# Edge sums by products with a matrix of the ends, all weights loaded at once, and a score behind layer 2's operands, in a kernel of four graph layers

## The chip, the cores and the metric

The kernel runs on one core of one Trainium2 chip; no other core runs a part of it. The metric is device time in microseconds (us) of one launch; less is better. Every comparison below sets runs of a kernel against runs of the kernel before on the same chip, taken in the same rounds.

Engines, as the profile names them: PE is TensorE's products, PEld its weight loads, DVE is VectorE, ACT is ScalarE, POOL is GpSimd, SP issues DMAs.

## The reference, cut to what matters

128 graphs of 128 nodes with 256 features pass four layers; each adds its result to its input and normalizes. All is float32. Layer 0 is attention along 512 edges, and the change's first part is in it:

```python
Xq = (H @ W_lin.T).reshape(bt, n, h, dh)
Qs = Xq[:, src]                     # the queries of each edge's one end
Kt = Xq[:, dst]                     # and of its other end
e = jnp.einsum('behd,hd->beh', leaky_relu(Qs + Kt, 0.2), a)
e = e + jnp.log(A0[src, dst] + EPS)[None, :, None]
...                                 # softmax over the edges of each source
Y = segment_sum(attn[..., None] * Vt, src, num_segments=n)
```

Layer 1 is three products by weights w1, w2, w3, each followed by a mixing of the nodes. Layer 2 is the change's third part: three weights for the diagonal, the upper and the lower part of the adjacency.

```python
h = jnp.einsum('bjf,kfo->kbjo', x, W)
out = adj_0 @ h[0] + adj_1 @ h[1] + adj_2 @ h[2] + bias
```

Layer 3 is two products with batch norms over all graphs.

## The kernel before: the parts that matter

The graphs go in 32 quads of four, through a software pipeline. A function `start` brings the first quads to the point where the pipeline is full; then each iteration does the attention of one quad, layer 1 of an earlier one, layers 2 and 3 of one earlier still. The order of the calls is the order in each engine's queue, and an operation waits for those in front of it there: in the prediction below, an operand whose input is there at 372.4 us is made at 375.67, after the score that stands before it.

A score of one chunk of 128 edges is three VectorE passes over 128x1024, 3.65 us together. Its input, the sum of the queries at both ends, comes by two gathers from the quad's queries in HBM, the second with an add:

```python
def gather_one(k, t, c):
    s = quads[k]
    idx, op = ((src_idx, ALU.bypass), (dst_idx, ALU.add))[t]
    nc.gpsimd.indirect_dma_start(out=s.z[c], ..., in_=s.qd, in_offset=...idx[:, c:c + 1]..., compute_op=op)

def score(k, c):
    ...
    nc.vector.scalar_tensor_tensor(z, z, SLOPE, z, op0=ALU.mult, op1=ALU.max)
    nc.vector.tensor_mul(z3, z3, a_bc...)
    nc.vector.reduce_sum(s.es[:, c, :], ...)
    if c == NE - 1:
        nc.vector.tensor_add(s.es, s.es, log_col...)
```

The edges are sorted by source for the softmax's scans: `perm` is a 0/1 matrix of the sorting, and the sorted indices are products with it. The gathers use those, so they have to wait for them.

The attention of a quad is scattered to HBM and read back as a matrix `ad`; `by_row` copies it into the order that the aggregation's products need, by ScalarE or, in the start, by ScalarE and VectorE in turn:

```python
def by_row(k, j, copy=None):
    ...
    (copy or nc.scalar.copy)(s.adc[:, j * H:(j + 1) * H, :],
                             s.ad.rearrange("p (s r) -> p r s", r=R)[:, j * H:(j + 1) * H, :])
```

Layer 2 is a generator. Its operands (`mix`: two products, one ScalarE copy, and `ms`, a VectorE multiplication) are made for one graph at a time, its products (`prod`) follow:

```python
mix(0)
mix(1)
yield
prod(0)
yield
mix(2)
prod(1)
yield
mix(3)
layer_norm(...)
prod(2)
yield
prod(3)
layer_norm(...)
```

The first step (up to the first `yield`) is taken at the end of the iteration before. An iteration then takes two more steps, a score, and the rest, so that the score stands between `prod(1)` and `mix(3)`:

```python
parts = quads[a].layer2 if a > 0 else iter(())
next(parts, None)
next(parts, None)
if has_e:
    score(e, 0)
    gather_last(e)
for _ in parts:
    pass
```

Of the kernel before, what the change touches and what calls it, by code (L numbers as in the profile page):

```python
# [8 lines left out]
F32 = mybir.dt.float32  # L9
# [16 lines left out]
def gnn_stack(ctx: ExitStack, tc: tile.TileContext, x, adj, w_qv_t, a, w_out_t, src, dst,  # L26
# [101 lines left out]
    with ExitStack() as phase:  # L128
        cst = phase.enter_context(tc.tile_pool(name="cst", bufs=1))

        class Quad:
            pass

# [107 lines left out]

        def values(k, i, copy=None, queue=None):

            copy = copy or nc.vector.tensor_copy
            s = quads[k]
            if i == 0:
                s.qt = wk.tile([P, QB, D], F32, tag="xb", name=f"qt{k}", bufs=1)
                s.xv = ws.tile([P, QB, D], F32, tag="xv", name=f"xv{k}", bufs=3)
            pq = ps("pq")
            for c in range(DC):  # L250
                nc.tensor.matmul(pq, s.xts[i // 2][:, i % 2, c, :], wqv[:, c, :], start=(c == 0), stop=(c == DC - 1))
            nc.scalar.copy(s.qt[:, i, :], pq[:, :D])
            copy(s.xv[:, i, :], pq[:, D:])
            if i == QB - 1:
                spill(k, queue)

        def spill(k, queue=None):
            s = quads[k]
            s.qd = q_dram[k % 4]
            (queue or nc.sync).dma_start(s.qd, s.qt.rearrange("p b d -> p (b d)"))  # L260

# [46 lines left out]

        def gather(k, z=None, chunks=range(NE - 1)):


            s = quads[k]
            s.z = z or {}
            for c in chunks:
                if c not in s.z:
                    s.z[c] = z_buffer(k, c)
            jobs = [(t, c) for t in range(2) for c in chunks]
            if k == 0:
                jobs = [(0, 0), (0, 1), (1, 0), (0, 2), (1, 1), (0, 3), (1, 2), (1, 3)]
            for t, c in jobs:  # L320
                gather_one(k, t, c)

        def z_buffer(k, c):
            return ws.tile([P, QB * D], F32, tag="zs", name=f"zs{k}_{c}", bufs=NE - 1)
# [12 lines left out]

        def score(k, c):

            s = quads[k]  # L340
            if c == 0:
                s.es = ws.tile([P, NE, R], F32, tag="es", name=f"es{k}", bufs=1)
            z = s.z[c]
            nc.vector.scalar_tensor_tensor(z, z, SLOPE, z, op0=ALU.mult, op1=ALU.max)  # L344
            z3 = z.rearrange("p (b d) -> p b d", d=D)
            nc.vector.tensor_mul(z3, z3, a_bc.unsqueeze(1).to_broadcast([P, QB, D]))  # L346
            nc.vector.reduce_sum(s.es[:, c, :], z.rearrange("p (r d) -> p r d", d=DH), axis=AX.X)  # L347
            if c == NE - 1:
                nc.vector.tensor_add(s.es, s.es, log_col.unsqueeze(2).to_broadcast([P, NE, R]))

        def softmax_parts(k):

            s = quads[k]
            pe = ps("pe")
            for c in range(NE):
                nc.tensor.transpose(pe[:R, c * P:(c + 1) * P], s.es[:, c, :], ident)
            f = wk.tile([R, E], F32, tag="f", name="f", bufs=1)
# [431 lines left out]
        def iteration(k):  # L789
# [6 lines left out]
            parts = quads[a].layer2 if a > 0 else iter(())  # L796
            next(parts, None)
            next(parts, None)
            if has_e:
# [143 lines left out]
        def start():  # L943
# [24 lines left out]
            adj_idx = wk.tile([P, NE], I32, tag="adj_idx", name="adj_idx", bufs=1)  # L968
            nc.vector.scalar_tensor_tensor(adj_idx, ends[:, 0, :], float(N), ends[:, 1, :], op0=ALU.mult, op1=ALU.add)
            key_row = scratch("key_row")  # L970
            nc.vector.scalar_tensor_tensor(key_row, rows_i[0], float(E), pos, op0=ALU.mult, op1=ALU.add)
# [13 lines left out]

            quads[1].xr = load_x(1)
            nc.sync.dma_start(att_dram[0][:N * N, :].rearrange("(t s) r -> t (s r)", s=N), zero)
            nc.sync.dma_start(wo, w_out_t.rearrange("(c p) f -> p c f", p=P))
            values_in(0, quads[0].xr, nc.scalar.copy)
            for i in range(QB):  # L990
                values(0, i, nc.scalar.copy, nc.scalar)
            quads[2].xr = load_x(2)

            def sorted_columns(t):
                pc = ps("pcol")[:, :NE * 2].rearrange("p (c t) -> p c t", t=2)
                for c in range(NE):
                    for i in range(NE):
                        nc.tensor.matmul(pc[:, c, :], perm[:, i, c * P:(c + 1) * P], ends[:, t:t + 2, i],
                                         start=(i == 0), stop=(i == NE - 1))
                return pc  # L1000

            pc = sorted_columns(0)
            nc.vector.tensor_copy(src_idx, pc[:, :, 0])
            nc.vector.tensor_copy(dst_idx, pc[:, :, 1])
            gather(0, {NE - 1: l2w.rearrange("p k c f -> p (k c f)")[:, :QB * D]}, range(NE))
            pr = ps("src_row")
            for c in range(NE):
                nc.tensor.matmul(pr[:R, :], src_wide[:, c, :], perm[:, c, :], start=(c == 0), stop=(c == NE - 1))
            src_row = scratch("src_row")
            nc.scalar.copy(src_row[:R, :], pr[:R, :])  # L1010

            values_in(1, quads[1].xr, nc.scalar.copy)
            for i in range(QB):
                values(1, i, nc.scalar.copy, nc.scalar)
            z2 = zpool.tile([P, 2, QB * D], F32, tag="z", name="z_1", bufs=1)
            gather(1, dict(enumerate((z2[:, 0, :], z2[:, 1, :], w2t.rearrange("p c d -> p (c d)"),
                                      l3w1.rearrange("p c f -> p (c f)")))), range(NE))

# [16 lines left out]
            nc.vector.tensor_add(ends[:, 2, :], weight, pair_col)  # L1035

            pc = sorted_columns(2)


# [4 lines left out]

            xg3 = load_x(3, "xg", 1, ws)

            for c in range(NE):
                score(0, c)
                if c == 1:
                    nc.vector.tensor_copy(att_idx, pc[:, :, 0])  # L1050
                    nc.vector.tensor_copy(log_col, pc[:, :, 1])
            steps = softmax_parts(0)
            for _ in range(2):
                next(steps)
            values_in(2, quads[2].xr, nc.scalar.copy)
            next(steps)
            values(2, 0, nc.scalar.copy)
            values(2, 1, nc.scalar.copy)
            for _ in steps:
                pass  # L1060
            attention(0)
            for i in (2, 3):
                values(2, i, nc.scalar.copy)
            scatter(0)
            nc.sync.dma_start(w1_sb, w1.rearrange("(c p) f -> p c f", p=P))
            nc.sync.dma_start(w2_sb, w2.rearrange("(c p) f -> p c f", p=P))
            nc.sync.dma_start(att_dram[1][:N * N, :].rearrange("(t s) r -> t (s r)", s=N), zero)
            nc.sync.dma_start(w3_sb, w3.rearrange("(c p) f -> p c f", p=P))
            nc.sync.dma_start(l2w, l2_w.rearrange("k (c p) f -> p k c f", p=P))
            nc.sync.dma_start(bias, bass.AP(tensor=l2_bias.tensor, offset=l2_bias.offset, ap=[[0, P], [1, D]]))  # L1070
            for t, vecs in ((bn1, (l3_b1, l3_g1, l3_be1)), (bn2, (l3_b2, l3_g2, l3_be2))):
                for i, ap in enumerate(vecs):
                    nc.sync.dma_start(t[:, i, :], ap.rearrange("(c p) -> p c", p=P))

# [31 lines left out]

            values_in(3, xg3, nc.scalar.copy)
            gather(2)
            for c in range(NE - 1):
                score(1, c)  # L1110
            for j in range(QB):
                by_row(0, j, nc.vector.tensor_copy if j % 2 else None)
            aggregate(0)
            stage_a(0)
            for i in range(QB):
                values(3, i, nc.scalar.copy)
            quads[4].xg = load_x(4, "xg", 1, ws)
            score(1, NE - 1)
            nc.sync.dma_start(l3w1, l3_w1_t.rearrange("(c p) f -> p c f", p=P))
            nc.sync.dma_start(w2t, l3_w2_t.rearrange("(c p) f -> p c f", p=P))  # L1120
            mix1(0, 0)
            mix1(0, 2)
            steps = softmax_parts(1)
            first(0, 0)
            next(steps)
            second_sums()
            for i in range(QB):
                if i + 1 < QB:
                    first(0, i + 1)
                mix2(0, i)  # L1130
                next(steps, None)

        with tc.manual_schedule(engines=None):
# [305 lines left out]
```

## Time and profile before

| quantity | before |
|---|---|
| time, median of 3 runs | 3249.05 us (3248.92 to 3249.43) |
| span of the profiled run | 3252.2 us |
| TensorE busy | 3137.4 us, 96% |
| VectorE busy | 2145.3 us, 66% |
| ScalarE busy | 1276.3 us, 39% |
| TensorE waits for layer 2's operand `ms` | 33.9 us in 29 waits |

How to read it: with TensorE at 96%, anything that isn't TensorE's work can give back roughly the missing 115 us, and only if TensorE waits for it. It helps to cut the span into four parts by rows of TensorE's timeline. *Start* ends where the first row of the second product of layer 1 begins (109.99 us before). *Iteration 0* lasts until the same row of iteration 1. *Middle* lasts until the plain hidden products of the last quad. *Tail* is the rest, two batch norms whose code isn't touched. Before, the four are 109.99, 90.78, 2725.97 and 325.46 us.

The profile's lines that carry the argument are in the prediction below.

### The profile page before, as it was taken

To read this page: it belongs to the slowest core of one execution; us is meant where nothing else is said; L and a number is where in the kernel's file an instruction comes from. 1 tells how busy PE (TensorE), PEld (TensorE's weight loads), DVE (VectorE), ACT (ScalarE), POOL (GpSimd) and SP (SyncE) were. 2 spreads that over 40 slices of the span, in tenths; PEclk is the share of its full clock that TensorE was granted. 3 is DMA by queue.
4 is the path that set the end of the run, shared out by engine and by line. 5 is a ranking of instruction groups with operands and counts; after the bars stand their busy time and mean duration, and the time that the engine had idled before them with its cause. 6 is when DMAs were issued, how large, how long until landed. Compare 5 with 4: busy or idle time off the path is not lost. (4 is left out here: it accounts for less than half of the span.)

```text
span 3252.2 us, 41204 instructions
## 1 busy us (share of the span) xinstructions
PE 3137.4 (96%) x15884; PEld 2590.5 (80%) x15884; DVE 2145.3 (66%) x4200; ACT 1276.3 (39%) x2229; POOL 644.1 (20%) x541
## 2 busy tenths in 40 slices
PE   6999999999999999999999999999999999999997
PEld 3788888888888888888888888888888888874444
DVE  6666666666666666666666666666666666437878
ACT  2343333333333333333333333333333333326668
POOL 4211222212111111222112111112222111001125
PEclk7999999999999999999999999999999999999999
DMA  7613333333333223333333333233333331005557
GB/s 219 174 52 92 104 98 104 93 96 105 95 95 99 84 79 98 105 98 104 92 98 104 86 103 93 78 88 101 98 104 101 94 92 53 20 24 178 176 192 272
DMA packets 118756, 344.86 MB, mean 106 GB/s; under 512 B 15008, under 2 KB 51744, under 8 KB 110240
## 3 DMA queue, kind: packets, MB, share of 16 engines
q0 software_dynamic: 45552, 151.55, 19.4%
q1 hardware_dynamic: 70960, 188.71, 16.2%
q8 instruction: 126, 2.06, 0.3%
q10 hardware_dynamic: 2048, 1.97, 0.2%
q14 instruction: 70, 0.57, 0.1%
HBM read 256.20 MB, written 85.98 MB: 105 GB/s over the span
## 5 line engine op out<-in xcount | busy, mean ns | idle before, releaser
L535 PE MATMUL ph<-m,w 128*128 128x256 f32 x2048 | 464.2, 380 | 0.0
L616 PE MATMUL p<-w,h 128*128 128x256 f32 x2048 | 462.3, 379 | 0.0
L616 PEld LDWEIGHTS p<-w,h 128*128 128x128 f32 x2048 | 389.2, 190 | 65.9 <-issue 7.6
L535 PEld LDWEIGHTS ph<-m,w 128*128 128x128 f32 x2048 | 387.6, 190 | 51.4
L329 POOL DMA_INDIRECT zs<-qd,src_idx x123 | 119.6, 972 | 1443.7 <-DVE z L739 884.0
L666 PE MATMUL po<-l2w,ms 128*128 128x256 f32 x1536 | 355.7, 382 | 33.9 <-DVE ms L658 33.9
L535 PE MATMUL ph<-m,w_s 128*128 128x256 f32 x1536 | 352.4, 379 | 0.0
L666 PEld LDWEIGHTS po<-l2w,ms 128*128 128x128 f32 x1536 | 282.7, 190 | 78.7 <-DVE ms L658 45.4
L535 PEld LDWEIGHTS ph<-m,w_s 128*128 128x128 f32 x1536 | 291.9, 190 | 39.6
L112 ACT ACTIVATE ln_sd<-ln_mv,eps 128x2 f32<-128x2 f32 x192 | 56.3, 293 | 514.2 <-DVE ln_mv L107 514.1
L329 POOL DMA_INDIRECT zs<-qd,dst_idx x123 | 192.5, 1565 | 258.2 <-DMA zs<-qd,src_idx 246.9
L548 DVE TENSOR_TENSOR h<-ph,u 128x512 f32<-128x512 f32 x128 | 88.1, 689 | 167.6 <-PE ph L535 114.3
L389 POOL DMA_INDIRECT attd<-at,att_idx x128 | 126.1, 985 | 361.4 <-DMA attd<-at,att_idx 252.8
L542 ACT COPY u<-ph 128x512 f32<-128x512 f32 x128 | 74.9, 585 | 245.1 <-PE ph L535 245.1
L346 DVE TENSOR_TENSOR zs<-zs,a_bc 128x1024 f32<-128x1024 f32 x123 | 150.6, 1225 | 4.2
L347 DVE TENSOR_REDUCE es<-zs 128x16 f32<-128x1024 f32 x123 | 150.0, 1220 | 4.2
L344 DVE SCALAR_TENSOR_TENSOR zs<-zs 128x1024 f32<-128x1024 f32 x123 | 149.5, 1215 | 2.4 <-DMA zs<-qd,dst_idx 2.4
L120 DVE TENSOR_SCALAR xr<-xr,ln_mv,ln_rs 128x256 f32<-128x256 f32 x384 | 145.1, 420 | 6.9
L105 DVE BATCH_NORM_STATS2 ln_st<-xr 128x6 f32<-128x256 f32 x384 | 144.2, 417 | 5.5
L654 ACT COPY ms<-pm 128x512 f32<-128x512 f32 x128 | 71.1, 579 | 194.4 <-PE pm L652 191.0
L477 DVE TENSOR_TENSOR h<-z,adc 128x512 f32<-128x512 f32 x62 | 41.9, 675 | 153.9 <-ACT adc L471 153.8
L640 POOL TENSOR_TENSOR xb<-xr,bias 128x512 f32<-128x512 f32 x64 | 81.6, 1275 | 293.1 <-DVE xr L120 155.2
(298 smaller groups left out, 5706.9 us busy)
## 6 DMA issues: line engine op xcount, KB each, us to landing
ad<-attd SPq DMA_DIRECT2D x32, 1024.0 KB, 4.8
zd<-z SPq DMA_DIRECT2D x31, 1024.0 KB, 7.4
zl<-zd SPq DMA_DIRECT2D x62, 512.0 KB, 3.6
xr<-in_x_dram SPq DMA_DIRECT2D x32, 512.0 KB, 5.9
x3d<-xr SPq DMA_DIRECT2D x32, 512.0 KB, 5.4
x3l<-x3d SPq DMA_DIRECT2D x32, 512.0 KB, 5.1
out_dram<-x3l POOLq DMA_DIRECT2D x31, 512.0 KB
qd<-qt SPq DMA_DIRECT2D x30, 512.0 KB, 2.6
```

The costliest lines, as they stand in the source:

```text
L105: nc.vector.bn_stats(st[:, i, :], r[:, i, :])
L120: nc.vector.tensor_scalar(r[:, i, :], r[:, i, :], mv[:, i, 0:1], rs[:, i:i + 1], op0=ALU.subtract, op1=ALU.mult)
L329: nc.gpsimd.indirect_dma_start(out=s.z[c], out_offset=None, in_=s.qd, in_offset=bass.IndirectOffsetOnAxis(ap=idx[:, c:c + 1], axis=0), com ...
L344: nc.vector.scalar_tensor_tensor(z, z, SLOPE, z, op0=ALU.mult, op1=ALU.max)
L346: nc.vector.tensor_mul(z3, z3, a_bc.unsqueeze(1).to_broadcast([P, QB, D]))
L347: nc.vector.reduce_sum(s.es[:, c, :], z.rearrange("p (r d) -> p r d", d=DH), axis=AX.X)
L389: nc.gpsimd.indirect_dma_start(out=ad, out_offset=bass.IndirectOffsetOnAxis(ap=att_idx[:, c:c + 1], axis=0), in_=s.at[:, c, :], in_offset= ...
L535: nc.tensor.matmul(bank[g][:, i].rearrange("p b n -> p (b n)"), wa[:, c, f:f + P], s.m2[:, blk_b, c].rearrange("p b n -> p (b n)"), start= ...
L548: nc.vector.tensor_add(block(g, row, col), bank[g], kept_[g])
L616: nc.tensor.matmul(p3[:, t * D:(t + 1) * D], s.h2[f // 2][:, f % 2, j + t, :], w3_sb[:, f, :], start=(f == 0), stop=(f == K2 - 1))
L640: nc.gpsimd.tensor_add(s.xb[:, j:j + 2, :], xj, bias.unsqueeze(1).to_broadcast([P, 2, D]))
L666: nc.tensor.matmul(po[:, i % 2, :], mss[i][:, t, dc, :], l2w[:, t, dc, :], start=(n3 == 0), stop=(n3 == 3 * DC - 1))
```

## The change

Its intent: in the start, where nothing is in flight yet, TensorE is often idle, so let it build the edge sums of the first two quads with a product, in place of a spill, sixteen gathers and their latency. Have all weights loaded early, so that no later load stands in a queue. And in each iteration, make layer 2's next operand before the score, so that TensorE needn't wait for it.

The diff, cut to its core:

```diff
@@ iteration
             parts = quads[a].layer2 if a > 0 else iter(())
-            next(parts, None)
-            next(parts, None)
+            for _ in range(3):
+                next(parts, None)
             if has_e:
                 score(e, 0)
@@ new: edge sums by products, and sorting of the scores
+        def ends_sum(k, h, onehot):
+            s = quads[k]
+            for c in range(NE):
+                pz = ps("pz")
+                nc.tensor.matmul(pz, onehot[:, c * P:(c + 1) * P], s.qt[:, 2 * h:2 * h + 2, :], start=True, stop=True)
+                nc.scalar.copy(s.z[c][:, h * 512:(h + 1) * 512], pz)
+        def sorted_scores(k, perm):
+            s = quads[k]
+            s.pe = ps("pe")
+            for c in range(NE):
+                nc.tensor.matmul(s.pe[:R, :], s.es[:, c, :], perm[:, c, :], start=(c == 0), stop=(c == NE - 1))
@@ start
+            onehot = scratch("onehot")
+            nc.vector.tensor_scalar(onehot, rows_i[0], pos_col[:, 0:1], None, op0=ALU.is_equal)
+            nc.vector.scalar_tensor_tensor(onehot, rows_i[1], pos_col[:, 0:1], onehot, op0=ALU.is_equal, op1=ALU.add)
...                                  (all loads of weights and zeros moved up to here)
-            for i in range(QB):
-                values(0, i, nc.scalar.copy, nc.scalar)
...
-            gather(0, {...}, range(NE))
+            z_room(0)
+            for h in range(2):
+                for i in range(2):
+                    values(0, 2 * h + i, nc.scalar.copy)
+                ends_sum(0, h, onehot)
...                                  (quad 0's scores interleaved with quad 1's values)
             attention(0)
             scatter(0)
+            z_room(1)
+            for h in range(2):
+                ends_sum(1, h, onehot)
+            pc = sorted_columns(0)   (the sorted indices of the later gathers)
...                                  (adjacency: transposes, degrees, normalized matrix)
-            values_in(3, xg3, nc.scalar.copy)
-            gather(2)
-            for c in range(NE - 1):
-                score(1, c)
+            values_in(2, quads[2].xr, nc.scalar.copy)
+            for c in range(2):
+                score(1, c, ends[:, 3, :])
+            for i in range(QB):
+                values(2, i, nc.scalar.copy)
             for j in range(QB):
                 by_row(0, j, nc.vector.tensor_copy if j % 2 else None)
             aggregate(0)
...
```

`onehot` has a row for each node and a column for each edge, with a 1 at both ends of the edge, so one product with it gives both gathers and their sum. The edges are then in their first order, and the sorting moves to the scores, which are much narrower.

## The prediction

> **What bounds the kernel now.** I read the page's busy shares and slices first, then who waits for whom, then the timeline of one iteration of the middle, then that of the first 120 us.
>
> The page, its first lines and two of its slice rows:
>
> ```profile
> span 3252.2 us, 41204 instructions
> ...
> PE 3137.4 (96%) x15884; PEld 2590.5 (80%) x15884; DVE 2145.3 (66%) x4200; ACT 1276.3 (39%) x2229; POOL 644.1 (20%) x541
> ...
> PE   6999999999999999999999999999999999999997
> PEclk7999999999999999999999999999999999999999
> ```
>
> TensorE has work 96% of the span and full clock in all slices but the first. So 115 us (3252.2 - 3137.4) without TensorE work are all that hiding a wait can win, plus what a low clock costs at the start. Where do they lie? The waits, TensorE's own:
>
> ```profile
> PE po L666 <- DVE ms L658: 33.9, 29, 1.5
> PE pe L356 <- DVE es L349: 10.7, 1, 10.7
> PE py L416 <- ACT adc L402: 7.9, 1, 7.9
> ```
>
> The first is the only large wait that recurs (total, times, longest). The next two happen once, in the start. The timeline of the middle, VectorE and TensorE rows, shows how the first arises:
>
> ```profile
> 371.42 0.69 DVE L670 TENSOR_TENSOR xr<-xb,po 128x512 f32<-128x512 f32 x1 [2.24 <-PE po L666]
> 372.02 1.22 DVE L344 SCALAR_TENSOR_TENSOR zs<-zs 128x1024 f32<-128x1024 f32 x1
> ...
> 374.53 1.22 DVE L347 TENSOR_REDUCE es<-zs 128x16 f32<-128x1024 f32 x1
> 375.67 0.41 DVE L658 TENSOR_TENSOR ms<-pt,diag_bc 128x256 f32<-128x256 f32 x1
> 376.13 2.86 PE L666 MATMUL po<-l2w,ms 128*128 128x256 f32 x12 [1.15 <-DVE ms L658]
> ```
>
> The score of two quads ahead (3.65 us) stands in VectorE's queue before the operand that layer 2's last product needs, though the operand's own input was there at 372.4. TensorE waits 1.15 us, once an iteration. In the start (windows of 10 us: busy of each engine, then the granted clock) it is otherwise:
>
> ```profile
> 30.00:40.00 10.00, 6.86 (x33) 5.30 (x31) 5.18 (x11) 2.78 (x6) 3.79 (x4) 0.83 0.99 254
> 40.00:50.00 10.00, 1.34 (x7) 1.25 (x6) 9.83 (x11) 0.00 (x0) 7.40 (x6) 0.50 1.02 279
> 70.00:80.00 10.00, 1.12 (x8) 0.72 (x8) 9.83 (x9) 2.65 (x3) 5.33 (x7) 0.50 0.70 256
> 100.00:110.00 10.00, 7.85 (x41) 5.74 (x40) 8.54 (x11) 3.83 (x6) 0.00 (x0) 0.92 0.84 239
> ```
>
> VectorE does quad 0's scores in 40 to 50 and quad 1's in 70 to 80 while TensorE stands and loses half its clock. And these rows of the start's timeline are the marks against which I place the change:
>
> ```profile
> 36.92 1.21 DVE L344 SCALAR_TENSOR_TENSOR zs<-zs 128x1024 f32<-128x1024 f32 x1
> ...
> 71.89 0.34 SPq L392 DMA_DIRECT2D ad<-attd  x1
> 76.77 2.07 ACT L402 COPY adc<-ad 128x512 f32<-128x512 f32 x2 [6.17 <-DMA ad<-attd]
> 87.23 7.03 PE L251 MATMUL pq<-wqv,xt 128*128 128x512 f32 x16
> 94.09 1.95 PE L441 MATMUL pm<-wt_t,xr 128*128 128x128 f32 x16
> 109.99 4.51 PE L535 MATMUL ph<-m,w 128*128 128x256 f32 x16
> ```
>
> Scores begin at 36.9, attention 0 is back as a matrix at 76.8, and the second product of layer 1, from where TensorE stays nearly dense, begins at 109.99. That moment is what the first part of the change has to bring forward.
>
> **What the Trainium skill says.** (1) "TensorE: Matmul & The Clock Gate", The HAM clock gate: an idle array falls to half clock and needs about 3.4 us of work to get it back. The trace agrees: clock 0.50 in 40:50; at 52.0 work resumes and weight loads come 0.86 us apart until about 57, then 0.43. (2) The same page, Architectural detail: VectorE and ScalarE take their instructions in strict order. The 1.15 us above is just that. (3) "DMA: Bandwidth & Descriptors", Anatomy of one DMA: a DMA from GpSimd has a fixed cost near 2 us. Here each of the four dependent scatters of an attention takes 2.4 us (116.22, 118.67, 121.22, 123.60). (4) "ScalarE: Activation LUTs", Terms: a table load takes about 2.7 us; this trace has 1.28, which I use.
>
> **The change part by part.** A float32 product of 512 columns leaves two records; 16 of them take 7.03 us, so 0.43 us a record at full clock, 0.86 at half.
>
> *Layer 2's operands before the score.* Removes the recurring wait. In the window 200:2900 it is 32.7 us in 28 times; the 29th lies in iteration 0, which is not edited. After it the operand is made at about 372.5 + 0.4, well before the third product ends at 374.98. The score then ends near 378.8 instead of 375.7, the second layer norm starts after it at about the old time, and VectorE is at most 1 us later against TensorE than now, where it later idles 2.4 us (before 404.08). The last gather, started by that score, comes 3 us later: issue of its second half at 383 instead of 380.3, use at 393; a landing of 5 us fits. Worth: **-32.7 us**.
>
> *Products instead of gathers.* Removes 16 gathers, two spills and their latency. Adds 2 quads x 2 halves x 4 chunks = 16 products = 32 records: 13.8 us of TensorE; 16 ScalarE evictions of 128x512 at 0.58 = 9.3 us; two VectorE comparisons for the matrix (about 1.2 us). Sorting now happens on the scores, 2 x 4 products = 16 records, 6.9 us, in place of eight transposes (1.02 and 0.60 us for four). Together TensorE gets +19 us in the start, where it is busy for 77 of 110 us now. My placing of the queues in their new order, with durations from the rows above:
> - the matrix waits for the second row of ends (5.5 to 6.6 us after issue, so 9.1). Quad 0's sums run interleaved with its queries: 12.4 to 23.5. ScalarE reaches Ln at 25.8, scores begin at **26.6** (before 36.9): 10.3 us won.
> - Four scores at 3.8 with the small add, and between them casts and reset rows (1.8): end 43.7 (before 51.7). Sorting the last chunk to 45, scans to 48.2. The exponential stands behind the values of quad 1 in ScalarE's queue and a table load: 51. Attention 0 at about **55** (before 61.1): 6 us.
> - Scatter 0.5 + 9.7, load 4.9: matrix at **70** (before 76.8): still 6.7.
> - But meanwhile TensorE does quad 1's sums (54 to 63, cold at first), the sorted indices (3.6, 66.7), and only then the adjacency chain (4.6 us long at 64.06 to 68.66 now; then about 71.5), and the queries of quad 2 (to 81.6). VectorE idles some 11 us before the indices. The row copies of attention 0 stand behind quad 2's in ScalarE's queue: 82.5. Aggregation starts at **83.6** (before 77.9 to 80.2): 3.5 us lost.
> - Layer norm ends at 93.5 (91.5). Quad 3's transposed copies stand behind its square roots in ScalarE, so its values run 93.3 to about 100 (before 87.2 to 94.1). First mixing at **100.5** (before 94.1).
> - After it: mixing 2, first products 7.1, sorting 3.4, second mixing 3.7, 116.7; before, the same stretch took 15.9 with a wait of 2.2. So the second product starts near **117**, 7 us later than 109.99. With full clock throughout it would be 112.5.
>
> *Weights at once.* About 8.7 MB at the 240 to 290 GB/s of these windows: done around 40 us. TensorE has no wait for a weight now, so worth 0. The sums of w2 (4 x 1.22 us on VectorE) move behind the second mixing and can hold the fifth block of that product for about 1.3 us.
>
> Sum of the start: +7 + 1.3, less about 2 because I may have counted too much cold clock: **+6**. Total: 3249 - 32.7 + 6 = **3222 us**.
>
> **The rivals.**
> 1. The start wins after all. For it: gathers gone, scores 10 us earlier, and TensorE idle for 33 of the first 110 us. Its floor: 77 + 19 = 96 busy us, some 8 fewer at full clock, and 5 before the first data: 93, 17 us below now. Then 3249 - 32.7 - 17 = 3199. Against it: the queues in the new order have long unrelated work in front of the critical row copies.
> 2. The wait in the middle only changes its place: the later score delays the last gather or the layer norm, and TensorE waits for a score or for a bank instead. Then 3249 + 6 = 3255. Against it: the slack counted above, and no other TensorE wait recurs with VectorE at 67%.
> 3. Weights, zeros and x in one burst delay the small early loads and the four gathers of weights. The use at 23 us leaves 10 us. At worst 5 us more: 3227.
>
> **Range and chances.** The middle is nearly sure within 3 us; the start lies between -10 and +15. So 3206 to 3236. Faster by 2% needs 3184, below even rival 1's floor; slower by 2% needs 65 us more, which only an unseen recurring wait could give.
>
> **What would show it.** Middle: the row of the last product waiting for the operand goes from 29 times to about one and no new TensorE row of some 30 us takes its place. Start: scores at 26 to 28, the row copies of attention 0 bound by ScalarE's queue rather than by the DMA, and the second product of layer 1 at 112 to 120. If that begins before 108, my placing of quad 2's queries or of the clock is wrong; if the attention matrix comes later than 76, the exponential or the scatters are.

## The result, and the profile after

Ratios in this document are the mean time of one kernel's fast runs over that of the other's in the same rounds, so they are not quite the ratio of the medians that stand beside them.

The changed kernel took 3224.95 us (median of 4, 3222.49 to 3228.62) against 3248.99 us; the ratio is 0.9927 with a 95% interval of 0.991 to 0.9944. That is the same within 2%, and 24 us less. A word of care on the spans of the two profiles, 3252.2 and 3220.8 us: the profiled run was among the slower of the kernel before (3253.91 us) and the fastest of the changed one, so their difference of 31.4 us is larger than that of the medians. I therefore compare parts of the span, and over several runs.

The page of the changed kernel, first lines:

```profile
span 3220.8 us, 41286 instructions
## 1 busy us (share of the span) xinstructions
PE 3150.9 (98%) x15924; PEld 2601.2 (81%) x15924; DVE 2146.7 (67%) x4208; ACT 1286.3 (40%) x2245; POOL 637.7 (20%) x525
```

TensorE has 13.5 us more to do and still the span is shorter: the gap between the two shrank from 115 to 70 us. TensorE's waits say where. Code after the edits sits 10 to 14 lines lower, so the former L666 is L680 now (total, times, longest):

```profile
PE pt L1352 <- ACT agg L1194: 7.4, 4, 3.3
...
PE po L680 <- DVE ms L672: 1.2, 1, 1.2
```

The wait for `ms` went from 29 times to one (at 2879.29 us, in the last quad's layer 2, where the operand waits for a layer norm and no score is called), and no other takes its place: the largest wait is now one of the tail, four times. The timeline in the middle shows the new order, to be set beside the one in the prediction:

```profile
380.75 3.62 PE L680 MATMUL po<-l2w,ms 128*128 128x256 f32 x16
...
380.96 0.42 DVE L672 TENSOR_TENSOR ms<-pt,diag_bc 128x256 f32<-128x256 f32 x1 [0.33 <-PE pt L671]
...
383.48 1.22 DVE L354 SCALAR_TENSOR_TENSOR zs<-zs 128x1024 f32<-128x1024 f32 x1
```

VectorE makes the operand at 380.96, as soon as its input is there, and the score follows at 383.48. TensorE goes from one product to the next without a mark of idle time (its row is cut short here, at the end of the window that was read, 384 us).

Now the start. Windows of 10 us of the changed kernel (each engine's busy time and count, then the granted clock, DMA share and GB/s):

```profile
20.00:30.00 10.00, 10.00 (x42) 5.29 (x40) 6.41 (x15) 4.40 (x7) 0.00 (x0) 0.93 1.05 399
30.00:40.00 10.00, 10.00 (x29) 5.18 (x28) 9.79 (x15) 2.46 (x6) 0.00 (x0) 0.73 0.47 124
40.00:50.00 10.00, 5.21 (x12) 1.55 (x10) 6.19 (x7) 2.67 (x6) 0.00 (x0) 1.00 0.00 0
60.00:70.00 10.00, 8.81 (x44) 6.33 (x42) 1.17 (x6) 4.21 (x6) 2.19 (x4) 0.81 0.29 107
70.00:80.00 10.00, 8.14 (x22) 4.90 (x23) 8.79 (x17) 2.67 (x7) 0.00 (x0) 0.68 0.00 1
```

The two holes of TensorE at 40 and at 70 us are partly filled: 5.21 and 8.14 us of ten, before 1.34 and 1.12. In their place VectorE is nearly without work from 60 to 70. The rows of VectorE show both ends of this:

```profile
25.73 1.22 DVE L354 SCALAR_TENSOR_TENSOR zs<-zs 128x1024 f32<-128x1024 f32 x1
...
54.32 0.22 DVE L397 TENSOR_TENSOR at<-rden,pat 128x64 f32<-128x64 f32 x1
...
67.76 0.16 DVE L1091 CAST src_idx<-pcol 128x4 int32<-128x4 f32 x1 [13.23 <-PE pcol L1055]
```

Scores begin at 25.73 (before 36.92) and attention 0 is done at 54.3 (before at 60.9). Then VectorE waits 13.23 us for the sorted indices, because these stand behind quad 1's edge sums in TensorE's queue. TensorE's rows from there:

```profile
53.62 9.95 PE L338 MATMUL pz<-qt,pos 128*128 128x512 f32 x16
63.40 4.33 PE L1055 MATMUL pcol<-ends,w_s 128*128 128x2 f32 x32
...
74.40 8.10 PE L251 MATMUL pq<-wqv,xt 128*128 128x512 f32 x16
84.19 2.08 PE L430 MATMUL py<-adc,xv 128*64 128x128 f32 x32 [1.70 <-ACT adc L416]
...
93.69 8.69 PE L251 MATMUL pq<-wqv,xt 128*128 128x512 f32 x16 [2.90 <-ACT xt L239]
102.22 1.95 PE L455 MATMUL pm<-wt_t,xr 128*128 128x128 f32 x16
...
118.38 3.62 PE L549 MATMUL ph<-m,w 128*128 128x256 f32 x16
```

and SP's request for the matrix of attention 0 with ScalarE's copies of it, whose row carries no wait and follows the last copy of quad 2's values:

```profile
48.61 1.28 ACT L379 ACT_TABLE_LOAD   x1
...
64.05 0.34 SPq L406 DMA_DIRECT2D ad<-attd  x1
...
82.80 0.38 ACT L253 COPY xv<-pq 128x256 f32<-128x256 f32 x1
83.06 2.06 ACT L416 COPY adc<-ad 128x512 f32<-128x512 f32 x2
```

The matrix of attention 0 was asked for at 64.05 us, 7.8 us earlier than before. But the copies of it start only at 83.06, where before they started at 76.77, held by the DMA. So 11.2 us won at the scores are 6.6 at the attention, and minus 6.3 at the row copies. The second product of layer 1 starts at 118.38 us, 8.4 us later than before.

### The profile page after: what moved, and what is told of

Read it like the earlier page. It is cut to its first block, busy times and chain, and to the rows that moved or that the text cites. A ratio compares the mean times of both kernels' runs of the same rounds, so it can differ in the third digit from the quotient of the medians.

```text
span 3220.8 us, 41286 instructions
## 1 busy us (share of the span) xinstructions
PE 3150.9 (98%) x15924; PEld 2601.2 (81%) x15924; DVE 2146.7 (67%) x4208; ACT 1286.3 (40%) x2245; POOL 637.7 (20%) x525
## 5 line engine op out<-in xcount | busy, mean ns | idle before, releaser
L680 PE MATMUL po<-l2w,ms 128*128 128x256 f32 x1536 | 348.5, 380 | 1.2 <-DVE ms L672 1.2
L680 PEld LDWEIGHTS po<-l2w,ms 128*128 128x128 f32 x1536 | 285.4, 191 | 36.0 <-DVE ms L672 1.5
L323 POOL DMA_INDIRECT zs<-qd,dst_idx x120 | 205.8, 1715 | 244.2 <-DMA zs<-qd,src_idx 234.5
L566 ACT ACTIVATE h<-h 128x512 f32<-128x512 f32 x192 | 121.4, 632 | 48.2 <-DVE h L562 48.2
```

Of the source, the lines that this page charges most:

```text
L323: nc.gpsimd.indirect_dma_start(out=s.z[c], out_offset=None, in_=s.qd, in_offset=bass.IndirectOffsetOnAxis(ap=idx[:, c:c + 1], axis=0), com ...
L566: nc.scalar.activation(h, h if src_ is None else src_, AF.Relu)
L680: nc.tensor.matmul(po[:, i % 2, :], mss[i][:, t, dc, :], l2w[:, t, dc, :], start=(n3 == 0), stop=(n3 == 3 * DC - 1))
```

## The experiments

My theory: the middle gained all (about 40 us), the start lost some 10, and it lost because the critical chain (row copies, aggregation) stands behind unrelated work in the engines' queues. The rivals: the middle is worth only the idle time that the profile lists (33 us) and the start lost little; or the start's loss comes from the burst of weight loads or from TensorE's added work. Times of the kernel before were 3252.08 us for e1, e2, e4, e5; 3251.74 us for e3, e6, e7 and e8; and 3252.01 us for e9. All kernels gave right results.

### e1: the middle alone

```diff
@@ kernel before, iteration
-            next(parts, None)
-            next(parts, None)
+            for _ in range(3):
+                next(parts, None)
```

> The kernel before with only the score of two quads ahead put behind layer 2's last operand. Theory (the middle is all of the gain and is worth more than the 32.7 us of idle time listed, about 40 us, because a stalled product also loses the overlap with its neighbours): 3249 - 40 = 3209 us, 3206 to 3212; each full iteration 1.4 to 1.5 us shorter; the start unchanged, second product of layer 1 at 110. Rival (the start gives a part of the gain and the middle exactly the listed idle time): 3216 us.

Measured: 3215.25 us (3213.74 to 3216.64), ratio 0.9884 [0.9869, 0.9899], which is 37.7 us less (0.0116 of 3252.08), give or take 5. (The 3206 to 3212 us expected were reckoned from a kernel before of 3249.) One wait is left, that of the last quad:

```profile
PE po L666 <- DVE ms L658: 1.2, 1, 1.2
```

By the total the two theories aren't told apart: it lies between them. By the part of the span they are: start and iteration 0 stayed (110.14 and 90.91 us, before 109.99 and 90.78), the middle went from 2725.97 to 2685.74 us, 40.2 less, and the tail, whose code is the same, took 2.7 us more. A full iteration, from second product to second product, takes 87.47 us (376.27 to 463.74) in place of 88.89 (378.83 to 467.72). What follows: this line is worth about 40 us in the middle, and it alone makes a faster kernel than the whole change.

### e7: the same wait taken away in the other direction

```diff
@@ kernel before, iteration
             next(parts, None)
-            next(parts, None)
             if has_e:
                 score(e, 0)
```

> The kernel before with the score of two quads ahead one step earlier, in front of layer 2's third operand, instead of later. Theory (the wait comes only from the score standing between an operand whose input is ready and a product that needs it at once; one step earlier the operand would be made at 371.6 and needed at 372.1): the recurring wait goes too, middle 2685 to 2690 us instead of 2726, time within 5 us of the one with the score later. Rival (the score must come after all operands, earlier only moves the wait to the third one): a wait of some 30 us at the operand stays.

Measured: 3212.93 us (3208.54 to 3213.95), ratio 0.9882 [0.9867, 0.9897], 38.4 us less; the middle 2685.75 us. The wait is again gone but for the last quad:

```profile
PE po L666 <- DVE ms L658: 1.3, 1, 1.3
```

Here the score comes *earlier*, not later, and the middle is the same to 0.01 us as in e1. So nothing is special about putting the score behind: what counted was that it stood between an operand and its input at the one moment at which TensorE had nothing else.

### e2: the start alone

```diff
@@ changed kernel, iteration
-            for _ in range(3):
-                next(parts, None)
+            next(parts, None)
+            next(parts, None)
```

> The changed kernel with the score put back in front of layer 2's last operand, so only the start is changed. Theory (the start loses 9 to 16 us): 3258 to 3265 us, the wait for the operand back at some 29 times and 34 us, second product of layer 1 at 118. Rival (the start wins): below 3249.

Measured: 3262.80 us (3261.27 to 3272.68), ratio 1.003 [1.0017, 1.0044], 9.8 us more than before (5.5 to 14.3). The wait is back, as the waits of this kernel show:

```profile
PE po L680 <- DVE ms L672: 33.6, 29, 1.3
```

and its middle is 2725.36 us. The start ends at 121.86 us. Theory held: the new start costs time.

### e3: layer 1's weights at once, alone

```diff
@@ kernel before, start
             for i in range(QB):
                 values(0, i, nc.scalar.copy, nc.scalar)
             quads[2].xr = load_x(2)
+            nc.sync.dma_start(w1_sb, ...)        (moved up from behind scatter(0))
+            nc.sync.dma_start(w2_sb, ...)
+            nc.sync.dma_start(att_dram[1]..., zero)
+            nc.sync.dma_start(w3_sb, ...)
```

These are only some of the loads that the change moves. Those of `l2w`, `w2t` and `l3w1` stay late: in the start of the kernel before, these tiles hold edge sums.

> The kernel before with the loads of layer 1's three weights and the second zeroing (4.5 MB) issued early, as in the change, and nothing else. Theory (weights are on no path, and early loads only compete with the gathers of quads 0 and 1, which the changed kernel no longer has): no gain; the gathers land later and the second product begins 5 to 15 us later than 110; time 0 to 15 us above the kernel before. Rival (early weights give part of the gain): 5 us or more below the kernel before.

Measured: 3261.45 us (3258.30 to 3263.11), ratio 1.0027 [1.0012, 1.0043], 8.8 us more; the second product starts at 115.14 us, 5.1 later. VectorE's rows of this kernel show how:

```profile
38.88 1.23 DVE L344 SCALAR_TENSOR_TENSOR zs<-zs 128x1024 f32<-128x1024 f32 x1 [1.96 <-DMA zs<-qd,dst_idx]
...
43.93 1.23 DVE L344 SCALAR_TENSOR_TENSOR zs<-zs 128x1024 f32<-128x1024 f32 x1 [1.31 <-DMA zs<-qd,dst_idx]
```

The scores, which before ran one after the other, now wait for their gathers: the four of quad 0 for 1.96, 1.31, 0.29 and 0.43 us. So in a start that gathers, the early burst costs time.

### e9: the changed kernel with its later weights late

```diff
@@ changed kernel, start
             quads[2].xr = load_x(2)
-            nc.sync.dma_start(w1_sb, ...)        (and zeros, w2, w3, l2w, bias, l3w1, w2t, norms)
             quads[3].xg = load_x(3, "xg", 1, ws)
...
             scatter(0)
+            nc.sync.dma_start(w1_sb, ...)        (the same list)
```

> The changed kernel with one part undone: the loads of the later weights and the zeros of the second attention array are issued after the scatter of attention 0 (as in the kernel before) instead of at once. Theory (this part is worth about nothing in the changed kernel, because the start's edge sums no longer come by gathers that the burst could delay): the second product of layer 1 begins within 3 us of the changed kernel's profiles (118.4 and 121.9), scores begin within 1 us of 25.7, and the ratio to the kernel before is between 0.991 and 0.994. Rival (the burst hurts here as it did when moved alone into the kernel before, by 5 us to the second product and 8.7 us of the total): second product near 113, ratio near 0.9895. Second rival (late loads collide with the read of the attention matrix or with the third quad's gathers): second product past 125, ratio over 0.995.

Measured: 3226.54 us (3225.80 to 3232.02), ratio 0.9921 [0.9908, 0.9935]; the second product starts at 121.91 us. Total and start are those of the changed kernel (e8 below: 0.9919 and 121.86). One expectation was missed: the scores begin at 27.84, not within 1 us of 25.73. That isn't the loads' doing, as TensorE's first rows of the changed kernel and of this one show:

```profile
6.81 4.33 PE L251 MATMUL pq<-wqv,xt 128*128 128x512 f32 x8
```

```profile
7.58 5.66 PE L251 MATMUL pq<-wqv,xt 128*128 128x512 f32 x8
```

The same eight records start 0.77 us later and take 1.33 us more, together the 2.1 us. A record is 0.43 us at full clock and 0.86 at half, and the weight loads come 0.86 us apart up to 11.15 us in e9 but only to 7.82 in the changed kernel, so the run of e9 merely had more of them at half. The Trainium skill's "TensorE: Matmul & The Clock Gate", section The HAM clock gate, says that the window over which activity is watched runs freely, so that one kernel shows different numbers of slow products from run to run; this agrees. What follows: with edge sums by products the burst is harmless, and moving the weights is worth 0 here. The burst runs at 399 GB/s from 20 to 30 us (window above), while nothing waits for a gather.

### e4: aggregation ahead of quad 2's queries

```diff
@@ changed kernel, start
+            for j in range(QB):
+                by_row(0, j, nc.vector.tensor_copy if j % 2 else None)
             values_in(2, quads[2].xr, nc.scalar.copy)
-            for c in range(2):
+            aggregate(0)
+            stage_a(0)
+            for c in range(3):
                 score(1, c, ends[:, 3, :])
             for i in range(QB):
                 values(2, i, nc.scalar.copy)
-            for j in range(QB):
-                by_row(...)
-            aggregate(0)
-            score(1, 2, ends[:, 3, :])
             gather(2)
-            stage_a(0)
```

> The changed kernel, but attention 0's row copies, its aggregation and the layer norm after it stand in the queues in front of quad 2's queries. Theory (the start is late because unrelated queries stand in front of the critical row copies): aggregation of quad 0 at about 75 instead of 84, second product at about 113 instead of 118.4, time about 5 us below the changed kernel's 3225: 3219 to 3222. Rival (TensorE's added work alone sets the end of the start): second product at 118 as before, 3225.

Measured: 3220.49 us (3217.53 to 3224.24), ratio 0.9899 [0.9884, 0.9914]; aggregation at 77.44 us (changed kernel 84.19), the second product at 115.02. Both are 2 us later than expected, but this profile was late before anything edited: quad 1's edge sums begin at 56.57 us, in the first profile of the changed kernel at 53.62. From there to the second product it takes 58.45 us in place of 64.76 (65.90 in e8). So the direction held: the same instructions, in another order, shorten the start by some 6 us. The total can't confirm it, because its interval overlaps those of the changed kernel (0.9919 [0.9906, 0.9933] in e8).

### e5: more of the queues reordered

```diff
@@ changed kernel, start
+            pc = sorted_columns(0)               (before quad 0's last scores)
+            adjt = ps("adjt_ps")[:, :N]
+            nc.tensor.transpose(adjt, a_sb, ident)
             for c in range(2, NE):
                 score(0, c, ends[:, 3, :])
...
             z_room(1)
-            for h in range(2):
-                ends_sum(1, h, onehot)
-            pc = sorted_columns(0)
+            ends_sum(1, 0, onehot)
...                                  (adjacency's VectorE work here, while softmax waits for ScalarE)
             attention(0)
             scatter(0)
+            ends_sum(1, 1, onehot)
+            nc.vector.tensor_copy(diag_bc, pd)
...
             nc.scalar.activation(sums[:, 4:5], sums[:, 3:4], AF.Sqrt)
```

> The changed kernel with the start's queues reordered: sorted indices and the transposed adjacency early, half of quad 1's edge sums between the exponential and the scans, the rest of the adjacency work spread over idle time, row copies after three of quad 1's scores. Theory (the products instead of gathers do pay, if the queues do not stall: TensorE idles some 25 us of the changed start): second product at 100 to 104 instead of 118.4 and 110 of before, time 3249 - 40 - 8 = 3201, 3195 to 3210. Rival (TensorE's added 19 us cannot be hidden): second product no earlier than 112, 3215 or more.

Measured: 3218.45 us (3211.53 to 3219.72), ratio 0.9889 [0.9873, 0.9904]; the second product at 110.91 us. That is better than the changed kernel, but well short of what I expected of start and total. A row of VectorE in this kernel names one reason:

```profile
61.71 0.16 DVE L1122 RECIPROCAL sums<-sums 128x1 f32<-128x1 f32 x1 [4.48 <-ACT sums L1120]
```

I had put the square root of the degrees behind the second half of quad 1's edge sums, whose copies fill ScalarE's queue. I had freed one queue and blocked another.

### e6: e5 with two calls moved

```diff
@@ e5, start
             scatter(0)
-            ends_sum(1, 1, onehot)
             nc.vector.tensor_copy(diag_bc, pd)
...
             nc.scalar.activation(sums[:, 4:5], sums[:, 3:4], AF.Sqrt)
+            ends_sum(1, 1, onehot)
...
             for i in range(QB):
                 values(2, i, nc.scalar.copy)
+            values_in(3, quads[3].xg, nc.scalar.copy)
...
             score(1, 3, ends[:, 3, :])
-            values_in(3, quads[3].xg, nc.scalar.copy)
```

> The reordered start once more, with the root of the adjacency degree in front of the second half of quad 1's edge sums on ScalarE, and quad 3's transposes before attention 0's rows. Theory: VectorE's idle time of 4.5 us before that root and TensorE's 3 us before quad 3's values go, the second product begins at 101 to 106 (111 in the first reordering, 118 in the change), time 7 us below the first reordering: about 40 + 6 us below the kernel before on this chip. Rival (something else sets the end of the start): second product at 110 or later.

Measured: 3210.86 us (3209.20 to 3215.25), ratio 0.9873 [0.9858, 0.9888], 41.3 us less than before (46 expected). TensorE's rows of this kernel:

```profile
75.10 3.68 PE L430 MATMUL py<-adc,xv 128*64 128x128 f32 x32 [6.06 <-ACT adc L416]
...
82.99 7.03 PE L251 MATMUL pq<-wqv,xt 128*128 128x512 f32 x16
...
106.02 3.62 PE L549 MATMUL ph<-m,w 128*128 128x256 f32 x16
```

The second product starts at 106.02 us, 4 us before that of the kernel before, with TensorE's added work still in. The values of quad 3 follow without a wait and at full clock. What is left, 6.06 us, is for the row copies of attention 0, and those now wait for the DMA:

```profile
74.00 2.01 ACT L416 COPY adc<-ad 128x512 f32<-128x512 f32 x2 [4.16 <-DMA ad<-attd]
```

This is the fastest of the kernels by its median: 14.7 us under the changed one of the same call (3225.56). Over e7, with its one deleted line, it is only 2.1 us ahead, and their intervals overlap. Nor do the parts of the span tell them apart: start and iteration 0 together take 197.25 us here, and with the old start 196.82 (e7), 200.77 (before) and 201.05 (e1). So e6 shows that the products can be had without a loss; that they gain anything over the gathers isn't shown.

### e8: the changed kernel again

Nothing is edited. It was run beside e3, e6 and e7, for a comparison on one chip.

> The changed kernel as it is, beside the others of this call on the same chip. Expected 27 us below the kernel before of the same rounds; second product of layer 1 at 118 to 122, the middle 2685.5, and the part after the last quad within 324 to 332, its spread not from the edit.

Measured: 3225.56 us (3224.19 to 3226.57), ratio 0.9919 [0.9906, 0.9933], 26.3 us less than before. The start ends at 121.86 us here.

### The parts of the span, all runs

From the rows named above, one profile each, in us:

| kernel | start | iteration 0 | middle | tail |
|---|---|---|---|---|
| before | 109.99 | 90.78 | 2725.97 | 325.46 |
| after | 118.38 | 92.62 | 2685.46 | 324.34 |
| after again (e8) | 121.86 | 92.82 | 2685.47 | 324.05 |
| after, weights late (e9) | 121.91 | 92.58 | 2685.87 | 329.94 |
| middle alone (e1) | 110.14 | 90.91 | 2685.74 | 328.11 |
| score earlier (e7) | 108.19 | 88.63 | 2685.75 | 324.23 |
| start alone (e2) | 121.86 | 93.90 | 2725.36 | 329.88 |
| weights early (e3) | 115.14 | 92.83 | 2725.36 | 328.07 |
| rows first (e4) | 115.02 | 90.57 | 2685.45 | 331.46 |
| reordered (e5) | 110.91 | 91.79 | 2685.45 | 329.85 |
| better (e6) | 106.02 | 91.23 | 2686.27 | 329.98 |

The middle takes two values, with the wait and without, whatever the start is. The tail moves by 7 us with no edit in it. It goes with TensorE's granted clock in that part: 0.98 or 0.99 in the four profiles of 324 to 325.5 us, 0.95 to 0.97 in the seven of 328 us and more. What sets the clock there isn't shown, and this is the reason not to read a few us out of a total.

## Why the prediction was right or wrong

The total was right: 3222 us predicted, 3224.95 measured, inside the range. That it came within 3 us was luck: two sizes were off by about 8 us each, in opposite directions.

**The wait in the middle: mechanism right, size too small.** The term of -32.7 us measured -40.5 (2725.97 to 2685.46), 1.45 us in each of the 28 iterations in place of 1.15 to 1.17. The middle had been called nearly sure within 3 us. I took the listed idle time for the cost. TensorE's rows before, next to the one with the wait that the prediction shows, tell what was missed:

```profile
368.55 2.76 PE L666 MATMUL po<-l2w,ms 128*128 128x256 f32 x12
371.14 1.03 PE L652 MATMUL pm<-split_t,xr 128*128 128x256 f32 x4
...
372.23 2.76 PE L666 MATMUL po<-l2w,ms 128*128 128x256 f32 x12
...
378.83 5.34 PE L535 MATMUL ph<-m,w 128*128 128x256 f32 x24
```

A group of twelve records is listed with 2.76 us, but the next one starts 2.59 us after it (371.14 - 368.55): the end of a row overlaps the start of the next. So without the wait the product would have followed 372.23 at 374.82. It started at 376.13, 1.31 us late. And after it the next group came at 378.83, 2.70 us later in place of 2.59, another 0.11. Together 1.42 us, as much as a full iteration got shorter in e1 (88.89 to 87.47), and close to the 1.45. Seen over the whole middle, TensorE's time without work fell by 33.1 us (41.85 to 8.77), and its busy time by another 7.4 (2684.12 to 2676.69) with the same 14271 products. The work that I counted as possible harm, the later gather and the later layer norm, cost nothing: no such wait recurs.

**The start: order of events right, cost too small.** Nearly all marks fell where they were placed: scores at 25.73 and 26.57 us in the two profiles of the changed kernel (26.6 predicted), attention 0 at 54.3 and 56.7 (55), the row copies by ScalarE's queue at 83.06 and 85.02 (82.5), aggregation at 84.19 and 86.16 (83.6). That the copies would stand behind quad 2's in ScalarE's queue, and not wait for the DMA, is what the profile shows. But from there on I was too hopeful. Quad 3's values were to take from 93.3 to 100; they ran from 93.69 to 102.2 and, in e8, from 95.65 to 105.7, partly at half clock (8.69 and 10.20 us for sixteen records that take 7.03 at full clock), after a wait of 2.9 us for their transposed copies. The second product came at 118.38 us and, in e8 and e2, at 121.86 (117).

The step that failed is the discount: "less about 2 because I may have counted too much cold clock". There was more cold clock, not less. Taking the middle one of three profiles of each start (109.99 of 108.19, 109.99, 110.14; 121.86 of 118.38, 121.86, 121.86), the start lost 11.9 us, and iteration 0 another 1.8 (90.78 to 92.62; 1.3 predicted, with VectorE's sums of w2 named as its cause). TensorE waits there 0.78 us for an operand behind those sums and 0.83 for a score. So the term of +6 measured about +14 by the parts, and +9.8 (5.5 to 14.3) by the total of e2. With the middle: -40.5 + 13.7 = -26.8, against -23.7, -26.3 and -25.7 by the three ratios (first result, e8, and e9, in which only the loads differ).

Four readings of the prediction need correction, though the total doesn't hang on them. The 29th wait for the operand isn't in iteration 0 but in the last quad (2909.57 us before). A 9 in the row of the clock means 90% or more of a long slice, not full clock: the windows 150 to 160 and 160 to 180 us had 0.81 and 0.75. Work resumes at 52.0 us and the clock is back at about 57, which is 5 us (the first 2.5 of them transposes) and not the 3.4 that stand beside it. And the middle within 3 us and a start of -10 to +15 give 3203 to 3234 us, not 3206 to 3236.

**Weights at once: 0, right for this kernel.** e9 shows no difference. e3 shows that a burst can delay gathers, as the third rival has it, but there it is those of the edge sums, in a kernel that still has them in its start; the four gathers of the edges' weights that the rival named held up nothing here.

**The rivals.** The first, that the start wins after all, fell for this kernel, and its argument against was the right one: e4 changes only the order of queues, e5 and e6 almost only that (an intermediate matrix gets a place of its own), and e6 makes the start end at 106.02 us with the same products. So it wasn't TensorE's added work that lost the start. The second, that the wait only changes its place, fell with e1 and e7. That each of the queue moves does what its mechanism says is shown by the rows; how the 16 us between 121.9 and 106.0 divide among them isn't, since e5 moved several at once and e6 two.

## What to carry to other kernels

A small recurring wait on the bounding engine can be worth more than its listed idle time: measure it from start to start of the products on either side, and multiply by its count. Before adding work to fill an idle engine, ask which queue the critical operation stands in and what will be ahead of it there; a result that comes 7 us earlier is worth nothing if its consumer is queued behind other copies. When a change of several parts comes out ahead, run each part alone: here one moved line was worth more than the whole.

## What the Trainium skill lacked or had wrong

- No page says how the listed idle time of TensorE relates to what a wait costs: 1.15 us were listed, 1.42 us lost by the start-to-start times, and 1.45 us by the change of the whole middle over 28 iterations.
- "TensorE: Matmul & The Clock Gate", The HAM clock gate, ties the low clock to an array that isn't busy enough. Not said is whether many narrow products count as such. In the kernel before, 32 products with two columns, back to back in 3.6 us, were followed by a fall: the weight loads of the next products, which wait for nothing else, come 0.43 us apart at first (19.05 to 19.48) and 0.86 a little later (21.03 to 21.89):

```profile
19.05 0.10 PEld L1008 LDWEIGHTS src_row<-w_s,src_wide 128*16 128x16 f32 x1 [0.33 <-issue]
19.48 0.10 PEld L1008 LDWEIGHTS src_row<-w_s,src_wide 128*16 128x16 f32 x1 [0.33 <-issue]
...
21.03 0.15 PEld L1008 LDWEIGHTS src_row<-w_s,src_wide 128*16 128x16 f32 x1 [0.70 <-issue]
21.89 0.15 PEld L1008 LDWEIGHTS src_row<-w_s,src_wide 128*16 128x16 f32 x1 [0.70 <-issue]
```

  That the narrow products caused it is likely but wasn't tried alone.
- "ScalarE: Activation LUTs", What ACT_TABLE_LOAD costs, gives about 1.28 us for the load and 1.38 for a drain. The load agrees (1.28 us at 48.61); the exponential starts 1.30 us after the load did, at 49.91, so no drain shows behind it here, nor in front, where the copy before the load ends at 48.60. The 2.7 us of the page's Terms, which the prediction set aside, would have been too much.
